# Layer 0 of a two-layer macaron kernel: the product delta times u on GpSimd, in four pieces of 256 columns

## The chip, the cores and the metric

The kernel runs on one core of a Trainium2 chip. A core has five engines with a queue each: TensorE (PE; its weight loads are shown as PEld), VectorE (DVE), ScalarE (ACT), GpSimd (POOL) and SyncE (SP), which here issues DMA transfers. Each engine takes the instructions of its queue in order and waits, with everything behind, until what the next instruction needs is ready. The metric is the device time of one launch in microseconds (us); less is better. Times of single instructions come from one execution that the hardware profiler recorded.

## The reference

Input `x` has 4 sequences of 1024 tokens with 128 features. Layer 0 is a mixture of experts, a selective state-space block and the mixture again; layer 1 is a mixture, an attention with 16 modulations and the mixture again. The part that matters here is the state-space block of layer 0:

```python
u = jax.nn.silu(u)                                  # after a convolution over 3 tokens
x_dbl = u @ W_x
dt, Bm, Cm = jnp.split(x_dbl, [DT_RANK, DT_RANK + D_STATE], axis=-1)
delta = jax.nn.softplus(dt @ W_dt + b_dt)
deltaA = jnp.exp(jnp.einsum('bld,dn->bldn', delta, A))
deltaB_u = jnp.einsum('bld,bln->bldn', delta * u, Bm)
...
h = dA * h + dbu                                    # along the 1024 tokens
y = jnp.einsum('bdn,bn->bd', h, c)
...
y = y + u * D_param
```

There are 4 sequences `b`, 256 inner features (two halves `c` of 128, one per partition) and 16 states `n`. The product `delta * u` depends on `b` and `c` only; it is made eight times and used by 16 states each.

## The kernel before

All of layer 0 is written under a manual schedule: the order in which the Python code issues instructions is the order in every queue. The work is cut into small generators ("pieces"), and a loop of 128 ticks, one for each (b, c, n), advances each piece a step and then does the recurrence of its tick.

A tick `t` consists of these steps, all on tiles of 128 partitions and 1024 columns (tokens):

- `inflow(t)`, GpSimd, L484: `hs = du * row_b`, in four operations of 256 columns. It is issued `AHEAD` = 5 ticks ahead by `total`, and `hs` has six buffers, so an `hs` can be written once PE has read the tile of six ticks ago. Behind it SP loads the row of `Bm` for tick t + 3, spread over 128 partitions (512 KB).
- `decay(t)`, ScalarE, L493: `da = exp(delta * A)`, into the one PSUM tile of that name; it has to wait until the scan of the tick before has read it.
- `state(t)`, VectorE: the scan L499 along the tokens (reads `da` and `hs`), then L503, the product with the row of `Cm`; SP loads the next such row behind it.
- `total(t)`, PE, L512: adds `hs` to the sum `y` over the 16 states, through a product with the identity.
- `skip(b, c)`, VectorE, L523, after the 16 states: `u * D + y`.

Between the ticks run the other pieces. `mixtures` computes the mixture of experts, one expert a step: PE makes `hp` (L359), ScalarE `r` (L325), GpSimd multiplies `r` by the routing weights `m_w` in two operations of 256 columns (L332), ScalarE squares it to `h` (L342), PE multiplies `h` by the second weights (L349). Where a tick advances that piece twice, two of each stand there. `others` does gates and routing; its `route_rows` and `normed` are chains of small VectorE operations on 8 columns (`rsqrt`, L81 to L87). `following` prepares the next sequence: `prepare(b)` makes `u`, and `softplus(b, c)` makes `delta` in steps of ScalarE and VectorE (L432 to L460) and ends with `du` (L461). For the second half c = 1 it waits until the last tick of the sequence before. `following` is advanced before `mixtures`, and both before `total` and `state` of the tick.

For the first sequence both `softplus(0, 0)` and `softplus(0, 1)` run before the loop, beside the mixture of sequence 1; after them the first five `inflow` and the first `decay` are issued, then the ticks.

`delta` and `du` have two buffers each. `delta` is read by `decay` and by the product `du`; `du` is read by `inflow` alone. GpSimd's queue in layer 0 holds L332, L484, the gate products L538, and some fills at the start.

Of the kernel before, what the change touches and what calls it, by code (L numbers as in the profile page):

```python
# [22 lines left out]
ALU = mybir.AluOpType  # L23
# [4 lines left out]
B, L, C = 4, 1024, 128  # L28
# [132 lines left out]
def layer0(tc, k):  # L161
# [15 lines left out]
    nc = tc.nc  # L177
# [11 lines left out]
    with (  # L189
# [194 lines left out]
        u, x_rows, xd, delta, du = {}, {}, {}, {}, {}  # L384
# [41 lines left out]
        def softplus(b, c):  # L426


            v = sb.tile([P, L], F32, name="sp_v", bufs=1)
            for half in range(3):  # L430
                if half > 0:
                    nc.scalar.activation(  # L432
                        v[:, ts(half - 1, HL)], pdt, AF.Identity, bias=k.b_dt[:, c : c + 1]
                    )
                if half < 2:
                    pdt = ps_t.tile([P, HL], F32, name="pdt", tag="tr")
                    nc.tensor.matmul(
                        pdt,
                        k.w_dt[:, ts(c, P)],
                        xd[b][0:DTR, ts(half, HL)],  # L440
                        start=True,
                        stop=True,
                    )
                yield
            z = sb.tile([P, L], F32, name="sp_z", bufs=1)
            nc.vector.scalar_tensor_tensor(z, v, -1.0, v, op0=ALU.mult, op1=ALU.min)
            yield
            nc.scalar.activation(z, z, AF.Exp)
            yield
            w1 = sb.tile([P, L], F32, name="sp_w", bufs=1)  # L450
            nc.vector.tensor_scalar(w1, z, 1.0, None, op0=ALU.add)
            nc.vector.scalar_tensor_tensor(z, w1, -1.0, z, op0=ALU.add, op1=ALU.subtract)
            yield
            nc.scalar.activation(w1, w1, AF.Ln)
            nc.vector.scalar_tensor_tensor(v, v, 0.0, z, op0=ALU.max, op1=ALU.subtract)
            yield
            yield from until(lambda: c == 0 or now >= b * DI * NS - 1)
            delta[b, c] = sb.tile([P, L], F32, name="delta")
            du[b, c] = sb.tile([P, L], F32, name="du")
            nc.vector.tensor_tensor(delta[b, c], v, w1, op=ALU.add)  # L460
            nc.vector.tensor_tensor(du[b, c], delta[b, c], u[b][:, c, :], op=ALU.mult)  # L461
            yield


# [120 lines left out]
        def until(ready):  # L585
            while not ready():
                yield
# [26 lines left out]
        def following():  # L614

            for b in range(1, B):
                yield from until(lambda: now >= (b - 1) * DI * NS and {1, b} <= mixed)
                yield from prepare(b)
                yield from softplus(b, 0)
                yield from softplus(b, 1)  # L620

        def first():
            yield from prepare(0)
            yield from softplus(0, 0)
            yield from softplus(0, 1)
# [972 lines left out]
```

## Time and profile before

| what | value |
|---|---|
| device time, median of 3 runs | 8004.84 us (8004.07 to 8005.69) |
| profiled execution, device time | 8007.9 us |
| its span, first to last instruction | 8006.1 us |
| granted TensorE clock, mean | 0.963 |
| PE, DVE, ACT, POOL busy share of the span | 84%, 86%, 91%, 11% |
| first and last start of a scan's decay (L493) | 162.4 and 945.2 us |
| L484 on GpSimd, 512 operations: min, median, max | 712, 723, 1795 ns |
| L461 on VectorE, 8 operations: min, median, max | 1226, 1594, 1633 ns |
| L460 on VectorE, 8 operations: min, median, max | 1218, 1628, 1744 ns |

The span is the profiled execution's time from its first to its last instruction; the device time of the same execution has the launch around it. A row of costly groups gives the source line, the engine, the operation, the tile written and the tiles read, the number of instructions, then busy time in us and the mean of one in ns, and last the idle time of the engine just before them with what ended it. A row of the timeline gives the start in us, the length in us, the engine, the line and the operation; operations that follow each other without a gap are merged and counted ("x4"), and a bracket shows idle time before and what ended it. A row of the waits gives the waiting engine with its tile and line, what it waited for, then the total in us, the number of times and the longest. The eight `delta` (L460) start at 146.5, 161.7, 315.3, 370.6, 515.0, 577.3, 710.1 and 758.8 us. Busy time by stretches of 100 us:

| stretch, us | PE | DVE | ACT | POOL |
|---|---|---|---|---|
| 100 to 200 | 66.41 | 50.61 | 50.21 | 58.31 |
| 300 to 400 | 77.24 | 84.29 | 53.84 | 81.29 |
| 500 to 600 | 77.06 | 79.96 | 56.97 | 80.56 |
| 700 to 800 | 74.27 | 81.18 | 54.55 | 81.99 |
| 1200 to 1300 | 85.15 | 88.92 | 100.00 | 2.40 |

### The profile page before, as it was taken

The page shows a single profiled execution, that of the slowest core. Times are in us where ns is not written, and L with a number is a line of the kernel's source. Part 1 is how long each engine was busy: PE and PEld are TensorE (multiplying, and loading weights), DVE is VectorE, ACT ScalarE, POOL GpSimd, SP SyncE. Part 2 cuts the span into 40 slices and gives each one's busy share as a digit, 9 for nine tenths or more (in the row PEclk, how much of TensorE's full clock was granted, in tenths as well). Part 3 has the DMA queues.
Part 4 walks back from the last instruction along what each step waited for, and adds up shares of the span by engine and source line. Part 5 has one row for each costly group of instructions (what it writes and reads, how often), then busy time and mean ns, then how long its engine had stood idle before and what let it go on. Part 6 is the DMA issues. An engine that isn't in the chain of part 4 may idle for free. (4 is left out here: it accounts for less than half of the span.)

```text
span 8006.1 us, 169674 instructions
## 1 busy us (share of the span) xinstructions
PE 6750.8 (84%) x76154; PEld 3048.4 (38%) x76154; DVE 6919.1 (86%) x11239; ACT 7292.7 (91%) x1800; POOL 863.6 (11%) x1025
## 2 busy tenths in 40 slices
PE   6777778888888888888888888888888888888885
PEld 3443343333333333333333333333333333333333
DVE  4878668898988999888899898888899989888886
ACT  4555449999999999999999999999999999999995
POOL 4777610000000000000000000000000000000000
PEclk8988879999999999999999999999999999999997
DMA  3556400000000000000000000000000000000001
GB/s 118 193 190 195 155 27 1 2 1 1 2 2 1 2 2 1 2 2 2 1 2 1 2 2 2 1 2 2 1 1 1 2 1 2 1 2 1 2 1 32
DMA packets 71789, 192.09 MB, mean 24 GB/s; under 512 B 9848, under 2 KB 19840, under 8 KB 71040
## 3 DMA queue, kind: packets, MB, share of 16 engines
q1 hardware_dynamic: 66736, 178.38, 6.9%
q8 instruction: 604, 9.90, 0.5%
q10 hardware_dynamic: 4304, 2.62, 0.1%
q14 instruction: 145, 1.19, 0.0%
HBM read 176.91 MB, written 4.06 MB: 23 GB/s over the span
## 5 line engine op out<-in xcount | busy, mean ns | idle before, releaser
L1276 ACT ACTIVATE p_w<-xs,cc 128x7680 f32<-128x7680 f32 x1024 | 6747.8, 6713 | 23.3 <-PE o L1287 23.3
L1287 PE MATMUL o<-p_w,vt 128*9 128x256 f32 x61440 | 3791.6, 385 | 777.0 <-ACT p_w L1276 776.1
L1287 PEld LDWEIGHTS o<-p_w,vt 128*9 128x9 f32 x61440 | 1772.2, 92 | 2723.4 <-ACT p_w L1276 1216.5
L1062 DVE TENSOR_REDUCE nm<-s 128x1 f32<-128x1024 f32 x512 | 624.5, 1220 | 281.8 <-PE s L1048 280.6
L1114 DVE SCALAR_TENSOR_TENSOR x_m<-p_s,x_m 128x512 f32<-128x512 f32 x1024 | 708.5, 692 | 35.6
L1115 DVE SCALAR_TENSOR_TENSOR x_m<-x_m,p_s 128x512 f32<-128x512 f32 x1024 | 708.6, 692 | 34.9
L1116 DVE SCALAR_TENSOR_TENSOR p_s<-x_m,x_z 128x512 f32<-128x512 f32 x1024 | 708.5, 692 | 34.9
L1113 DVE SCALAR_TENSOR_TENSOR p_s<-x_m 128x512 f32<-128x512 f32 x1024 | 700.7, 684 | 0.0
L1085 DVE COPY xs<-s 128x1024 f32<-128x1024 f32 x508 | 608.4, 1218 | 98.5 <-PE s L1048 98.2
L1143 POOL TENSOR_TENSOR rz<-rz,iw_c 128x128 f32<-128x128 f32 x64 | 26.0, 407 | 5732.9 <-DVE rz L1142 5732.9
L1287 PE MATMUL o<-p_s,vtop 128*9 128x256 f32 x4096 | 623.5, 383 | 9.7 <-DVE vtop L1124 9.7
L1048 PE MATMUL s<-kp,qp 32*128 32x512 f32 x2048 | 581.4, 644 | 0.7 <-DVE nm L1062 0.7
L1048 PE MATMUL s<-qp,kp 32*128 32x512 f32 x2048 | 549.4, 634 | 0.8 <-ACT xs L1085 0.8
L1101 DVE TENSOR_SCALAR x_z<-xs,cc 128x512 int32<-128x512 f32 x1024 | 522.7, 510 | 1.1
L1105 DVE TENSOR_SCALAR x_m<-x_z 128x512 int32<-128x512 int32 x1024 | 437.7, 427 | 35.3
L1108 DVE TENSOR_SCALAR x_z<-x_z 128x512 int32<-128x512 int32 x1024 | 437.6, 427 | 35.3
L484 POOL TENSOR_TENSOR hs<-du,row_b 128x256 f32<-128x256 f32 x512 | 438.1, 888 | 112.3 <-PE y L512 103.2
L499 DVE TENSOR_TENSOR_SCAN hs<-da,hs 128x1024 f32<-128x1024 f32 x128 | 292.2, 2283 | 89.9 <-ACT da L493 74.4
L512 PE MATMUL y<-hs,ident 128*128 128x512 f32 x512 | 287.6, 692 | 97.1 <-DVE hs L503 71.3
L1319 DVE COPY os<-o 128x512 f32<-128x512 f32 x512 | 348.7, 681 | 10.1 <-PE o L1287 9.1
L1132 PEld LDWEIGHTS pt<-ident,os 128*128 128x128 f32 x2048 | 214.2, 140 | 368.2 <-issue 118.8
L493 ACT ACTIVATE da<-delta,neg_a 128x1024 f32<-128x1024 f32 x128 | 142.7, 1115 | 229.1 <-DVE hs L499 228.7
(228 smaller groups left out, 4343.9 us busy)
## 6 DMA issues: line engine op xcount, KB each, us to landing
row_b<-x_rows SPq DMA_DIRECT2D x128, 512.0 KB
row_c<-x_rows SPq DMA_DIRECT2D x128, 512.0 KB
m_w<-m_rows SPq DMA_DIRECT2D x128, 256.0 KB
x_sb<-in_L_attn_x_dram ACTq DMA_DIRECT2D x4, 512.0 KB
c_w<-in_L_ffn_w_dram SPq DMA_DIRECT2D x4, 512.0 KB
out_dram<-x_sb SPq DMA_DIRECT2D x4, 512.0 KB
c_b<-in_L_ffn_b_dram SPq DMA_DIRECT2D x2, 512.0 KB
xnt<-xs SPq DMA_DIRECT2D x2, 512.0 KB
```

The source lines that it names most:

```text
L484: nc.gpsimd.tensor_tensor(hs[t][:, part], du[b, c][:, part], rows_b[t][:, part], op=ALU.mult)
L1048: nc.tensor.matmul(s[:, ts(half, 512)], a[row, ts(i, P)], c[row, ts(half, 512)], start=True, stop=True,)
L1062: nc.vector.tensor_reduce(nm[:, i, 0:1], score(j, qp[n], i, kp[n]), AX.X, ALU.max, negate=True)
L1085: copy(xs[u][:, i, :], score(j, kp[n], i, qp[n]))
L1101: nc.vector.tensor_scalar(z, s, c, 127.0 * (1 << 23), op0=ALU.mult, op1=ALU.min)
L1105: nc.vector.tensor_scalar(m, z, 0x7FFFFF, 0x3F800000, op0=ALU.bitwise_and, op1=ALU.bitwise_or)
L1113: nc.vector.scalar_tensor_tensor(w, m, EXP2[0], m, op0=ALU.add, op1=ALU.mult)
L1114: nc.vector.scalar_tensor_tensor(m, w, EXP2[1], m, op0=ALU.add, op1=ALU.mult)
L1115: nc.vector.scalar_tensor_tensor(m, m, EXP2[2], w, op0=ALU.add, op1=ALU.mult)
L1116: nc.vector.scalar_tensor_tensor(p_s[g][:, 0:n], m, EXP2[3], e, op0=ALU.add, op1=ALU.mult)
L1276: nc.scalar.activation(p_w[:, n_s - min(SOFT) :], xs[u].rearrange("p a b -> p (a b)")[:, n_s:], AF.Exp, scale=cc[:, h, wl : wl + 1],)
L1287: nc.tensor.matmul(o[32 * r : 32 * r + D + 1, :], vtop[u] if soft else vts[b % 2][:, i, h, :], p_s[g][:, at : at + QW] if soft else p_w[:, ...
```

## The change

The product `du` leaves VectorE's queue and stands at the same place of the program on GpSimd, in four operations of 256 columns.

```diff
             delta[b, c] = sb.tile([P, L], F32, name="delta")
             du[b, c] = sb.tile([P, L], F32, name="du")
             nc.vector.tensor_tensor(delta[b, c], v, w1, op=ALU.add)
-            nc.vector.tensor_tensor(du[b, c], delta[b, c], u[b][:, c, :], op=ALU.mult)
+            for q in range(4):
+                part = ts(q, L // 4)
+                nc.gpsimd.tensor_tensor(
+                    du[b, c][:, part], delta[b, c][:, part], u[b][:, c, part], op=ALU.mult
+                )
             yield
```

VectorE's queue loses eight instructions and GpSimd's gains 32; the order of all others is the same on every engine. In GpSimd's queue the first `du` stands before the product of the last expert of sequence 1's mixture, and the second stands behind that product and before the first `inflow`. The `du` of c = 0 and c = 1 of the later sequences stand between the `inflow` of two ticks; at c = 1 of sequences 1 and 2 and at c = 0 of sequence 1 the products of two experts (L332) follow at once, at c = 1 of sequence 3 the product of one, and at c = 0 of sequences 2 and 3 an `inflow`. Lines after L461 lie four further down in the changed kernel, where the new product is L463.

## The prediction

> **What bounds the kernel now.** I read the page first, then the waits of 300 to 900 us, then the timeline around each of the eight places where `du` is made. The page puts the long stage after 1,200 us under ScalarE (L1276, 6747.8 us of 8006.1); the change does not touch it, and it starts when layer 0 is done. So only layer 0 counts, and in it the 128 ticks between 168 and 949 us.
>
> The costliest groups, two of them in layer 0 (busy, mean ns | idle before, releaser), and the line that goes:
>
> ```profile
> L484 POOL TENSOR_TENSOR hs<-du,row_b 128x256 f32<-128x256 f32 x512 | 438.1, 888 | 112.3 <-PE y L512 103.2
> L499 DVE TENSOR_TENSOR_SCAN hs<-da,hs 128x1024 f32<-128x1024 f32 x128 | 292.2, 2283 | 89.9 <-ACT da L493 74.4
> ```
>
> ```profile
> L461 DVE TENSOR_TENSOR du<-delta,u x8: 1226/1594/1633, 147.7 to 760.7; 128x1024 f32<-128x1024 f32 x8
> ```
>
> GpSimd runs ahead until the ring of six `hs` is full (it idles for PE `y`), so its product for a tick is early by about four ticks. VectorE idles most for the decay `da`, that is for ScalarE. What holds ScalarE up shows in the waits:
>
> ```profile
> ACT da L493 <- DVE hs L499: 181.4, 60, 8.9
> ...
> POOL hs L484 <- PE y L512: 80.0, 24, 8.6
> ...
> ACT h L342 <- POOL r L332: 49.8, 25, 4.4
> ...
> DVE hs L499 <- ACT da L493: 48.7, 18, 5.6
> ```
>
> The third row matters: ScalarE's queue is in order, `h` stands ahead of the next `da`, and `h` waits for GpSimd's product `r` (L332). A late GpSimd reaches the scan by r, h, da, scan, although its `hs` are early.
>
> **Prices.** A GpSimd product of 256 columns undisturbed takes 0.69 us (four in 2.77), a pair 1.40. VectorE's 1024-column product takes 1.23 alone; where the two meet, GpSimd's four take 3.75 (+0.98) and VectorE's one 1.4 to 1.74. Small VectorE operations show it best:
>
> ```profile
> 309.49 0.65 DVE L85 SCALAR_TENSOR_TENSOR rq<-rs 128x8 f32<-128x8 f32 x1
> ...
> 312.12 2.77 POOL L484 TENSOR_TENSOR hs<-du,row_b 128x256 f32<-128x256 f32 x4
> ...
> 314.26 0.65 DVE L86 TENSOR_TENSOR rq<-rq,tot 128x8 f32<-128x8 f32 x1
> 314.94 0.17 DVE L87 SCALAR_TENSOR_TENSOR rs<-rq,rs 128x8 f32<-128x8 f32 x1
> ```
>
> 0.65 us while GpSimd multiplies, 0.17 as soon as it stops: one small operation passes per GpSimd operation, 0.68 apart in place of 0.20, so 0.48 is lost on each.
>
> **The change, part by part.** Removed from VectorE: eight L461, 12.4 us in all. Added to GpSimd: 32 products, 32 x 0.69 = 22.2 us. Nothing else moves in any queue, and no DMA is added; but GpSimd's `du` now waits for `delta` (VectorE), and behind it wait the `r` and `hs` of the following ticks, and SP's loads of `row_b`, which follow `hs`.
>
> *Start (two places).* The rows, and the scan that follows:
>
> ```profile
> 151.26 22.75 POOL L484 TENSOR_TENSOR hs<-du,row_b 128x256 f32<-128x256 f32 x24
> ...
> 161.73 1.56 DVE L460 TENSOR_TENSOR delta<-sp_v,sp_w 128x1024 f32<-128x1024 f32 x1
> ...
> 163.32 1.63 DVE L461 TENSOR_TENSOR du<-delta,u 128x1024 f32<-128x1024 f32 x1
> ...
> 168.05 2.27 DVE L499 TENSOR_TENSOR_SCAN hs<-da,hs 128x1024 f32<-128x1024 f32 x1
> ```
>
> Six ticks of `hs` are made from 151 on, while VectorE is still busy with the second delta. In the new queue the second `du` stands before the first `hs`. The first `du` (149.1 to 151.9) delays the last `r` of the mixture, its `h` and ScalarE's work for the second delta by 2.0; with GpSimd then idle, four VectorE steps (L446, L452, L455, L460) fall from 1.52, 1.63, 1.63, 1.56 to about 1.22, -1.5. Delta ends at 163.85 (was 163.29), `du` at 166.65, the first `hs` at 169.45: the first scan at 169.5, +1.45. Then the lead is missing: eight `hs` blocks from 166.65 take 8 x 2.77 and 2 x 0.98 for two L503, to 190.8. The layer norm's 24 small VectorE operations (179.1 to 186.1 in the profile, 5 of them slow) now begin at 180.8 and meet GpSimd: 15 at 0.68 and 9 at 0.20 end at 192.8. Shift +6.7; after that both engines stand as before. Ends: +1.45 if none more is slowed, 1.45 + 19 x 0.48 = +10.6 if all are. I take 6.7, since the row at 309 to 315 shows exactly this. That loads of `row_b` come later (169.5 for use at about 176; in the profile 154.05 for 162.7) lies inside these ends.
>
> *Second halves, c = 1 (371, 577, 759 us).* The first of them:
>
> ```profile
> 370.23 4.74 POOL L484 TENSOR_TENSOR hs<-du,row_b 128x256 f32<-128x256 f32 x4
> ...
> 374.93 3.76 POOL L332 TENSOR_TENSOR r<-r,m_w 128x256 f32<-128x256 f32 x4
> ...
> 376.37 0.63 ACT L342 ACTIVATE h<-r 128x512 f32<-128x512 f32 x1 [3.48 <-POOL r L332]
> ...
> 376.90 1.10 ACT L493 ACTIVATE da<-delta,neg_a 128x1024 f32<-128x1024 f32 x1
> ```
>
> Here GpSimd is the late one. Without L461 its `hs` ends 0.98 earlier (373.99); `du` takes 2.77 and 0.98 for the L503 it meets, to 377.74; `r`, `h`, `da` come 2.8 later. VectorE is 1.6 early, waits for `da`, and starts its scan at 380.9 in place of 378.94; the skip after it (L523) waits for PE, which waits for `h`: +2.9. The place at 577 has the same rows: +2.9. At 759: `r` +2.8, scan +1.4, the next `r` and with it skip about +2.5. Sum +8.3 (2.0 to 2.9 each).
>
> *First halves, c = 0 (315, 515, 710 us).* Here GpSimd is early. At 515 and 710 it stands idle until delta, so the L503 and delta before it fall from 1.49 and 1.74 to 1.23; with L461 (1.63) gone the scan starts 2.3 earlier, `da` and the table loads behind it too; `du` and the late `hs` are four ticks ahead of need: -2.1 and -1.9. At 315, GpSimd idles from 309.4, the eight slow small operations save 8 x 0.48 = 3.8 and delta ends at 312.7; then `du`, two `r`, `hs` fill GpSimd to 322.1, the next `r` (321.76 in the profile) is no earlier, and of 1.8 only 0.7 stays. Sum -4.7 (ends -6.0, and 0 if `r` behind `du` eats all).
>
> Sum: 6.7 + 8.3 - 4.7 = **+10.3 us**; lower ends 1.45 + 6.0 - 6.0 = +1.5, upper 10.6 + 8.7 + 0 = +19.3. Against the profiled execution: span 8006.1 to 8016.4, with its launch (8007.9) to 8018.2; the median lies 3.1 under that, so 8004.84 + 10.3 = **8015.1**.
>
> The row prices four products at 2.77 us. The Trainium skill (GPSIMD Engine Reference, "Elementwise — side-by-side cycle accounting") gives 4.5 us for a product of 2048 columns, thus an estimate of 2.25 for 1024; with five `du` on the path (two at the start, three c = 1) the sum would be 5 x 0.52 lower, +7.7. No trace here shows one product of 1024 columns on GpSimd. The row of 3.75 beside 2.77 has a rule too (Trace Analysis, "Optimizing Scalar/DVE Operations"): GpSimd and VectorE share a port, and moving work between them may not help. Taken strictly it strikes out the gains at c = 0, and the sum is +15.0; the trace speaks against taking it so, since GpSimd stands idle there before delta.
>
> **Rivals.**
> 1. *GpSimd is the bound wherever it works for the experts, and pays in full.* Each of the six places in the loop costs 2.8, as `r` behind `du` holds ScalarE's `h` and `da`, and nothing of L461 comes back: 6 x 2.8 + 6.7 = +23.5, 8028. It decides as soon as `r` ends later than the scan that frees `da`. For it: 49.8 us of `h` waiting for `r`, and at 315 it eats most. Against: at 515 and 710 no expert product comes for 10 and 12 us (`r` at 526.95 and 728.29).
> 2. *VectorE is the bound, and GpSimd's lead hides all.* -12.4 for L461: 7992; with the slowed deltas and small operations (about -8) 7984. For it: 80.0 us of GpSimd waiting for `y`. Against: the start, where no lead exists yet, and the c = 1 rows.
> 3. *The change does nothing*, `du` being hidden both ways: 8005. Against: each c = 1 row has `h` waiting for GpSimd already.
>
> **How the numbers follow.** From no change this kernel can be told by about 0.2%, 16 us: 7988.8 and 8020.8. My sum 0.50 and rival 3 0.05, both within; rival 1 and mixtures near it 0.38 (slower); rival 2 0.07, of which 0.02 within and 0.05 faster. Same 0.57, slower 0.38, faster 0.05. The range runs from 8003, 3.5 below the lower end for some of rivals 2 and 3, to 8030, over rival 1; the forecast's own is 8006 to 8024.
>
> **What would show it.** Start: first scan near 169.5, the second layer norm's small operations at 0.65 until about 190, third scan near 192.8. At c = 1: `h` after `du` 2.8 later relative to delta's start, the scan waiting for `da`. At c = 0: GpSimd idle until delta, 1024-column delta at 1.23, the scan right behind it. Wrong if GpSimd's `du` are well above 0.69 each, if the third scan comes before 188, or if the c = 0 places lose time.

## The result, and the profile after

| | before | changed |
|---|---|---|
| median of 15 runs each, us | 8005.58 (7998.71 to 8011.31) | 8020.03 (8015.08 to 8024.63) |
| profiled execution, span, us | 8006.1 | 8018.2 |

The ratio is 1.0019, with a 95% interval of 1.0012 to 1.0025: 14.5 us slower, between 10 and 20. Forecast were +10.3 and a range of 8003 to 8030.

The same groups of the page, and the new line by its source (count: min/median/max in ns, first and last start):

```profile
L488 POOL TENSOR_TENSOR hs<-du,row_b 128x256 f32<-128x256 f32 x512 | 422.1, 857 | 109.8 <-PE y L516 108.0
...
L503 DVE TENSOR_TENSOR_SCAN hs<-da,hs 128x1024 f32<-128x1024 f32 x128 | 292.2, 2283 | 100.2 <-ACT da L497 82.6
```

```profile
L463 POOL TENSOR_TENSOR du<-delta,u x32: 712/722/1712, 148.4 to 774.5; 128x256 f32<-128x256 f32 x32
```

The 32 products cost what the row priced. The scan's idle time grew from 89.9 to 100.2 us, of it 82.6 for `da` (74.4 before). The waits of 300 to 900 us; the row of `h` was the point:

```profile
ACT da L497 <- DVE hs L503: 166.1, 57, 11.0
...
DVE hs L503 <- ACT da L497: 65.8, 23, 5.2
ACT h L342 <- POOL r L332: 63.1, 24, 7.1
...
POOL du L463 <- DVE delta L460: 10.1, 3, 3.4
```

`h` waits 13 us longer for `r`, the scan 17 us longer for `da`; the new wait is there, 10.1 us of GpSimd for delta, at the three c = 0 places alone.

**Where the time went.** I set the 128 scans of both traces side by side (start in the changed kernel less start before) and then four later points. Ticks count from 0. A "power" is one of the 1024 exponentials that ScalarE makes in the attention.

| point | shift, us |
|---|---|
| first scan; third scan | +1.1; +5.8 |
| tick 20; 25 (past sequence 1, c = 0) | +6.4; +4.5 |
| tick 36 (past sequence 1, c = 1) | +10.2 |
| tick 53; 55 (past sequence 2, c = 0) | +10.2; +8.2 |
| tick 64; 65; 68 (past sequence 2, c = 1) | +9.0; +15.6; +10.0 |
| tick 85; 90 (past sequence 3, c = 0) | +8.8; +6.4 |
| tick 95; 100 (past sequence 3, c = 1) | +5.3; +8.7 |
| last scan | +5.3 |
| first power of the attention (ScalarE, L1280) | +5.7 |
| end of its last | +3.2 |
| first layer-norm row of the last mixture (L95) | +9.7 |
| end of the span | +12.1 |

So less than half of the 12.1 us of these two profiles is in layer 0. Of the rest, 6.5 us arise between the end of the last power and the row of L95, in one wait of VectorE. (Another 2.4 arise behind that row, about what the attention had gained before it, 2.5; the second profile of the changed kernel, below, does not have them.) From VectorE's waits, before and changed:

```profile
DVE ln_st L95 <- issue: 2.4, 1, 2.4
```

```profile
DVE ln_st L95 <- issue: 8.9, 1, 8.9
```

"Issue" is time in which the engine waited for nothing that the profile shows. The two parts are taken one after the other.

**The start** went as worked out. The changed kernel's timeline:

```profile
163.66 2.77 POOL L463 TENSOR_TENSOR du<-delta,u 128x256 f32<-128x256 f32 x4 [11.11 <-DVE delta L460]
166.39 23.79 POOL L488 TENSOR_TENSOR hs<-du,row_b 128x256 f32<-128x256 f32 x32
169.19 2.29 DVE L503 TENSOR_TENSOR_SCAN hs<-da,hs 128x1024 f32<-128x1024 f32 x1 [2.42 <-POOL hs L488]
...
189.56 0.64 DVE L85 SCALAR_TENSOR_TENSOR rq<-ln_rstd 128x8 f32<-128x8 f32 x1
190.24 0.17 DVE L86 TENSOR_TENSOR rq<-rq,ln_a 128x8 f32<-128x8 f32 x1
...
191.92 2.28 DVE L503 TENSOR_TENSOR_SCAN hs<-da,hs 128x1024 f32<-128x1024 f32 x1
```

GpSimd multiplies without a gap to 190.18, and the layer norm's small operations run at 0.65 until just then.

**c = 1** did not. Sequence 1, around the skip (L527) that follows the second scan:

```profile
378.38 3.75 POOL L463 TENSOR_TENSOR du<-delta,u 128x256 f32<-128x256 f32 x4
...
382.09 2.77 POOL L332 TENSOR_TENSOR r<-r,m_w 128x256 f32<-128x256 f32 x4
383.52 0.63 ACT L342 ACTIVATE h<-r 128x512 f32<-128x512 f32 x1 [6.19 <-POOL r L332]
...
385.25 2.29 DVE L503 TENSOR_TENSOR_SCAN hs<-da,hs 128x1024 f32<-128x1024 f32 x1 [3.46 <-ACT da L497]
...
390.29 5.53 POOL L488 TENSOR_TENSOR hs<-du,row_b 128x256 f32<-128x256 f32 x8
390.55 1.28 DVE L527 SCALAR_TENSOR_TENSOR u<-u,c_d_param,y 128x1024 f32<-128x1024 f32 x1 [3.01 <-PE y L516]
...
391.75 5.14 DVE L507 TENSOR_TENSOR hs<-hs,row_c 128x1024 f32<-128x1024 f32 x1
```

`du`, `r`, `h`, `da`, scan is the predicted chain, with the predicted late scan. But then L507, 1.2 to 1.8 us at all but three ticks, takes 5.14. It ends at 396.89; GpSimd's unbroken eight products end at 395.82, 1.07 earlier. VectorE was held out until GpSimd paused. At tick 64 the same takes 7.06, at tick 96 4.33. In the kernel before, the same product at tick 32 took 1.71, also behind the skip with GpSimd at work, but at tick 96 it was long there too:

```profile
383.54 1.71 DVE L503 TENSOR_TENSOR hs<-hs,row_c 128x1024 f32<-128x1024 f32 x1
...
775.35 3.21 DVE L503 TENSOR_TENSOR hs<-hs,row_c 128x1024 f32<-128x1024 f32 x1
```

**c = 0** went as worked out. Sequence 2:

```profile
524.90 1.22 DVE L460 TENSOR_TENSOR delta<-sp_v,sp_w 128x1024 f32<-128x1024 f32 x1
...
526.04 2.28 DVE L503 TENSOR_TENSOR_SCAN hs<-da,hs 128x1024 f32<-128x1024 f32 x1
...
526.20 2.77 POOL L463 TENSOR_TENSOR du<-delta,u 128x256 f32<-128x256 f32 x4 [3.41 <-DVE delta L460]
```

Delta takes 1.22 (1.74 before), the scan is right behind it, GpSimd waits 3.41 for delta and delays nobody.

### The profile page after: what moved, and what is told of

It is laid out like the page before. It is cut to its first block, busy times and chain, and to the rows that moved or that the text cites. A ratio compares the mean times of both kernels' runs of the same rounds, so it can differ in the third digit from the quotient of the medians.

```text
span 8018.2 us, 169699 instructions
## 1 busy us (share of the span) xinstructions
PE 6751.3 (84%) x76154; PEld 3047.9 (38%) x76154; DVE 6911.2 (86%) x11231; ACT 7292.2 (91%) x1800; POOL 869.6 (11%) x1057
## 5 line engine op out<-in xcount | busy, mean ns | idle before, releaser
L1280 ACT ACTIVATE p_w<-xs,cc 128x7680 f32<-128x7680 f32 x1024 | 6747.9, 6694 | 20.8 <-PE o L1291 20.7
L503 DVE TENSOR_TENSOR_SCAN hs<-da,hs 128x1024 f32<-128x1024 f32 x128 | 292.2, 2283 | 100.2 <-ACT da L497 82.6
```

What stands on the lines that cost most here:

```text
L1280: nc.scalar.activation(p_w[:, n_s - min(SOFT) :], xs[u].rearrange("p a b -> p (a b)")[:, n_s:], AF.Exp, scale=cc[:, h, wl : wl + 1],)
```

## The experiments

There are three groups of four kernels, each group with its own 33 runs of the kernel before on the same chip. Times are differences between the median of 11 runs and the median of these 33; "last scan" is that scan's start in the run's profile less 946.4. Layer 0 is not the same to the microsecond in two executions, as the first experiment shows.

**The kernel before again**, no edit.

> The kernel before, unchanged, as a second profile and as the noise floor. If VectorE's wait before the last mixture's first L95 (2.4 us in the profile before, 8.9 in the changed kernel's) belongs to the program, it is 2.4 +- 1 here again and the time is within 4 us of before. If it is chance of an execution, it lies elsewhere in 2 to 9. In layer 0 every scan starts within 1 us of the profile before.

Time +2.1 us (ratio 1.0001, 0.9992 to 1.0010). The wait before L95 is 2.4 again. Layer 0 is less steady than expected: scans are within 2 us up to tick 68, then up to 4.9 late, and the last is 1.7 early. So a shift of under 5 us in the middle of layer 0 of one profile says nothing by itself, and one ratio of 11 runs leaves some 7 us either way. A step between two close ticks that recurs in several kernels says more. One such step is nobody's doing here: from tick 100 to the last scan this repetition loses 3.7 us, and all the other twelve profiles lose 0.7 to 3.7 as well, so that much of each "last scan" belongs to the first profile of before.

**One kind of place at a time.** The edit of the first kernel; the second has `b > 0 and c == 0` there, the third `b > 0 and c == 1`:

```diff
-            for q in range(4):
+            if b == 0:
+                for q in range(4):
...
+            else:
+                nc.vector.tensor_tensor(du[b, c], delta[b, c], u[b][:, c, :], op=ALU.mult)
```

> Only the two du of sequence 0 on GpSimd. Theory: the missing lead costs once, third scan at 191.9 in place of 186.1, and the 5.8 us stay to the end of layer 0 (last scan +5 to +7). Rival, the lead is regained and the loss with it: the shift is under 2 us by the 20th scan. Rival of rivals 1 (GpSimd is the bound and pays in full): 8 products add 5.5 on GpSimd and scans go on slipping after the third.

> Only the three du of c = 0 of sequences 1 to 3 on GpSimd. Theory: a gain at each, -2.0, -1.6, -1.9 us (as the changed kernel's scans show), together -5 to -6 at the last scan. Rival (GpSimd pays in full): +2.8 at each, +8.4. Third view, gains are given back at once by later waits: within 1.5 of zero.

> Only the three du of c = 1 of sequences 1 to 3 on GpSimd. Theory: h behind r behind du, and VectorE's L503 behind the skip held out while GpSimd multiplies without a gap: +5.4, +1.5, +1.8 where they happen, +6 to +9 at the last scan. The prediction's working: +2.9, +2.9, +2.5, +8.3, without a long L503. Rival (du is hidden): under 2 us.

| on GpSimd | time, us | ratio, interval | shift of scans |
|---|---|---|---|
| start alone | +5.2 | 1.0005, 0.9996 to 1.0014 | third +6.4, tick 94 +6.3, last +1.2 |
| c = 0 alone | -6.4 | 0.9990, 0.9981 to 0.9999 | tick 25 -1.1, 64 -5.5, 90 -7.7, last -13.3 |
| c = 1 alone | +12.9 | 1.0014, 1.0005 to 1.0023 | third 0.0, tick 36 +7.0, 68 +10.8, 100 +11.8, last +9.0 |

The signs are those of the theory, and those of the prediction. The start's loss holds for some 90 ticks; 2.7 of it is given back at tick 96, where the long product of before (3.21) is absent, and 2.4 in the last ticks, where every profile loses some; that only +1.2 is left there is against what I expected. Its time alone does not tell it from no change. c = 0 alone gains at each place (-1.9, -2.0, -1.7; in the seven other profiles with these three on GpSimd at the same places the steps are -1.5 to -2.5, in the repeated kernel before 0.1 at most). Its last scan is earlier than the theory allowed: of the -13.3, 5.6 are these places, 2.7 the long product of tick 96, absent here too, and 2.7 the last ticks; the rest is not accounted for, and the time shows -6. c = 1 alone has the long product each time (its line is L510 there, the skip's L530):

```profile
387.11 5.52 POOL L491 TENSOR_TENSOR hs<-du,row_b 128x256 f32<-128x256 f32 x8
388.24 1.28 DVE L530 SCALAR_TENSOR_TENSOR u<-u,c_d_param,y 128x1024 f32<-128x1024 f32 x1 [3.88 <-PE y L519]
389.44 4.27 DVE L510 TENSOR_TENSOR hs<-hs,row_c 128x1024 f32<-128x1024 f32 x1
```

The rival "GpSimd pays in full at each place" falls with c = 0, "hidden" with c = 1. The three times add to +11.7; all three kernels have the short wait before L95.

**Eight more VectorE instructions, in the changed kernel.**

```diff
             nc.vector.tensor_scalar(neg_a, neg_a, -1.0, None, op0=ALU.mult)
+            pad = cst.tile([P, NS], F32, name="pad")
+            for _ in range(8):
+                nc.vector.tensor_scalar(pad, neg_a[:, 0, :], -1.0, None, op0=ALU.mult)
```

> The changed kernel with eight small VectorE operations (16 columns, into a tile that nobody reads) ahead of the first mixture, so that VectorE has as many instructions as before. If the 8.9 us before the last mixture's first L95 come from where VectorE's instructions lie, the wait is 2.4 again and the time 4 to 7 us under the changed kernel's (+8 to +10 over before). If it comes from the moment or from chance, it is 8.9 or anything, and the time stays +14. The scans of layer 0 move by under 1.5 us, the start's by what the eight take.

Time +10.9 (1.0013, 1.0004 to 1.0022). The wait before L95 is 2.2. The shift of the scans differs from the changed kernel's by more than I had allowed (first scan +3.2 against +1.1, last +9.3), so the time is no clean measure. Whether the eight did that is not shown, as the changed kernel's second profile (below) has its first scan at +4.3 without them. The next attempt puts them behind the ticks.

**The skip behind the product**, in the changed kernel.

```diff
-            if t > 0 and tick[t][2] == 0:
-                skip(*tick[t - 1][:2])
             nc.vector.tensor_tensor(hs[t], hs[t], rows_c[t], op=ALU.mult)
+            if t > 0 and tick[t][2] == 0:
+                skip(*tick[t - 1][:2])
```

> The changed kernel, with the skip (L527) behind the product with row_c (L507) of the same tick instead of ahead of it. Theory: L507 was held out for 5.14, 7.06 and 4.33 us behind the skip at ticks 32, 64 and 96; ahead of the skip it takes 1.3 to 1.8, the skip, which reads PSUM, takes its 1.28 at once, and the time falls by 5 to 10 us against the changed kernel. Rival, the long L507 only fills a wait that ScalarE's da makes anyway: under 2 us, and the scans behind then wait for da.

Time +7.8 (1.0011, 1.0002 to 1.0020), against +14.5 and, repeated below, +12.6 of the changed kernel in other groups; last scan -3.3 against +5.3. The same stretch in its profile:

```profile
388.27 1.80 DVE L505 TENSOR_TENSOR hs<-hs,row_c 128x1024 f32<-128x1024 f32 x1
...
391.34 1.28 DVE L527 SCALAR_TENSOR_TENSOR u<-u,c_d_param,y 128x1024 f32<-128x1024 f32 x1 [1.28 <-PE y L516]
391.98 8.54 POOL L488 TENSOR_TENSOR hs<-du,row_b 128x256 f32<-128x256 f32 x11
```

The product (L505 in this kernel) takes 1.80, the skip its 1.28 at once though GpSimd multiplies, and no product in the run takes over 1.9. From tick 32 to 33 and from 64 to 65 the shift of the scans grows by less than 0.4, where it grows by 5.3 and 6.7 in the changed kernel. So the long product was on the path. By the medians the edit takes 5 to 7 us away; the intervals of the times overlap, so its size is not settled.

**The six later `du` behind the experts' products**, without and with that edit (`late` collects (b, c) where `softplus` made the product; sequence 0 is on VectorE).

```diff
...
             if now > 0:
                 total(now - 1)
+            while late:
+                product(*late.pop())
             state(now)
```

> The two du of sequence 0 on VectorE as before; the six later ones on GpSimd, but issued behind the experts' products and the inflow of their tick. Theory: without du ahead of r the c = 1 places lose nothing, and VectorE's 1.6 us come back: -2 at each of the six, -8 to -14 at the last scan. Rival (GpSimd's work costs wherever it stands, as it delays the next r by 2.8): +5 to +9 as with c = 1 alone.

> Both changes together. Theory: their gains add, -12 to -20 us against before. Rival, both remove the same wait: no better than the better of the two alone.

Time -1.3 (0.9998, 0.9989 to 1.0007) and -4.1 (0.9994, 0.9985 to 1.0003); last scan -3.4 and -8.2. Both miss: better than the changed kernel (the start's loss is out of both, too), but no clear gain on before. In the first, `du` at 378.71 stands ahead of the next tick's `r`, and that `h` waits 5.24: the delay was moved by a tick. That is the rival's mechanism, though its +5 to +9 did not come; and at tick 96 a product takes 6.49. In the second, no skip stands ahead of a product, yet the one behind the scan of tick 97 takes 6.54.

**The changed kernel again**, no edit, and **with eight VectorE instructions behind the ticks:**

```diff
         skip(B - 1, 1)
+        for _ in range(8):
+            nc.vector.tensor_scalar(neg_a[:, 0, :], neg_a[:, 0, :], -1.0, None, op0=ALU.mult)
```

> The changed kernel, unchanged, as a second profile. If VectorE's wait of 8.9 us before the last mixture's first L95 belongs to the program, it is 6 to 10 again, and from the end of the last decay-and-power activation of the attention to the end of the span it takes 6 to 9 us more than before; if it was chance, 2 to 3 in this one. Layer 0: last scan +3 to +8, the three long L507 again.

> The changed kernel with eight small VectorE operations behind the loop of ticks, on a tile that is no longer read, so that VectorE has as many instructions as before and the ticks are those of the changed kernel. Code theory: the wait before L95 is 2 to 3 and the time 5 to 8 us under the changed kernel's of this call. Rival, the wait depends on when the stage begins and not on the number of instructions: 6 to 10 as in the changed kernel.

Again: +12.6 (1.0017, 1.0008 to 1.0026); last scan +6.6, long products 4.96, 6.29, 4.15. With the eight: +8.6 (1.0011, 1.0002 to 1.0020); last scan +6.6 too. VectorE's wait in the one and in the other:

```profile
DVE ln_st L95 <- issue: 7.5, 1, 7.5
```

```profile
DVE ln_st L95 <- issue: 2.2, 1, 2.2
```

Over all fourteen profiles: 7.5, 7.6, 8.0 and 8.9 us in the four whose VectorE has 8 instructions fewer than before; 2.2 to 2.5 in the ten with 0, 2, 3 or 6 fewer, two of these being the changed kernel with eight put back at two different places. From the end of the last power to L95, the four take 4.1 to 6.5 us more than before; the two with eight put back, 0.2 less. In the other seven kernels with the short wait it differs from before by 0.2 at most. The time fell by 4.0 with the eight, less than the 5 to 8 expected, and within what two such medians differ by.

The Trainium skill (Runtime: NRT & Kernel Launch, "Instruction fetch mechanics") has an engine's instructions fetched in blocks of 256 while it executes, mostly hidden. A block that comes late would fit a wait that depends on the count, but no run here shows the fetch itself.

**One `du` in one piece**, in the changed kernel.

```diff
-            for q in range(4):
-                part = ts(q, L // 4)
-                nc.gpsimd.tensor_tensor(
-                    du[b, c][:, part], delta[b, c][:, part], u[b][:, c, part], op=ALU.mult
-                )
+            nc.gpsimd.tensor_tensor(du[b, c], delta[b, c], u[b][:, c, :], op=ALU.mult)
```

> The changed kernel with each du as one GpSimd operation of 1024 columns. By the rows (0.69 us for 256) it takes 2.7; by the page's 4.5 us for 2048 columns 2.25. If VectorE's two-input operations wait for the whole GpSimd operation that is running, L507 beside it waits up to 2.7 and GpSimd is not stretched to 3.75. Time within 5 us of the changed kernel's.

Time +8.5 (1.0012, 1.0003 to 1.0021), against +12.6 of the changed kernel in the same group; the intervals overlap. A piece takes 2.34 us, and VectorE's product beside it waits:

```profile
377.77 2.34 POOL L461 TENSOR_TENSOR du<-delta,u 128x1024 f32<-128x1024 f32 x1
378.09 3.10 DVE L503 TENSOR_TENSOR hs<-hs,row_c 128x1024 f32<-128x1024 f32 x1
```

0.32 us into GpSimd's operation, VectorE's (here L503) starts, and ends 1.08 after it: it waited for the whole. The Trainium skill (SBUF — State Buffer, "SBUF: two separate sides") says so: of a VectorE operation with two SBUF inputs and a GpSimd operation the first to start has the port pair for its whole length. This row agrees. By that rule alone four pieces would let VectorE in after at most 0.7 us; the 5.14 of L507 beside pieces of 0.69 does not agree. The 4.5 us that the Trainium skill (GPSIMD Engine Reference, "Elementwise — side-by-side cycle accounting") gives for 2048 columns is for an addition; half of it, 2.25 for 1024 as an estimate, is close to the 2.34.

This kernel also shows that standing behind the skip is not what decides. At tick 64 the product starts as far into GpSimd's operations as in the changed kernel, 0.87 and 0.88 us behind the start of the row, and behind the same skip. First the changed kernel, then this one:

```profile
598.52 2.77 POOL L488 TENSOR_TENSOR hs<-du,row_b 128x256 f32<-128x256 f32 x4
599.39 7.06 DVE L507 TENSOR_TENSOR hs<-hs,row_c 128x1024 f32<-128x1024 f32 x1
```

```profile
597.04 3.77 POOL L484 TENSOR_TENSOR hs<-du,row_b 128x256 f32<-128x256 f32 x4
597.92 1.62 DVE L503 TENSOR_TENSOR hs<-hs,row_c 128x1024 f32<-128x1024 f32 x1
```

Over all fourteen profiles a product behind the skip, with a GpSimd operation running as it starts and the next one following at once, was held out in 20 cases of 66, and behind a scan in one of some 1000 beside pieces of 256 columns.

**c = 0 alone, and the skip behind the product:** both edits above on one kernel.

> Only the three du of c = 0 of sequences 1 to 3 on GpSimd, and the skip behind the product with row_c. Theory: the gains of c = 0 stay (-6 to -13 at the last scan) and the long operation behind the skip at tick 96 of the kernel before (3.2 to 4.2) is gone: -8 to -16 us against before in the time. Rival: the skip's place was worth nothing there, as with the first halves alone (-6).

Time 7995.6, -10.6 us (0.9988, 0.9979 to 0.9997); last scan -12.2, no product over 1.9 us. It is the fastest of the kernels, and its whole interval lies under 1, as that of c = 0 alone just does. Against c = 0 alone (-6.4, another group) the intervals overlap, and that kernel has no product over 1.9 us either, its last scan at -13.3: there was no long product left for the moved skip to remove. That the move gains anything here is not shown.

## Why the prediction was right, and where not

The time lies in the range, 4.9 us over the point, and slower by 0.18%, inside the 0.2% that held most of the chance. The total is nearer than its steps.

- *Price of the 32 products, 0.69 us, and GpSimd's stretch to 3.75 beside VectorE:* as said (2.75 to 3.76 for four).
- *Start, +6.7:* right. First scan 169.19 (169.5 said), third 191.92 (192.8), the small operations slow until 190.2 (190.8). When the start was changed alone, the shift stayed to tick 96 (+6.3) and not to the end.
- *c = 0, -4.7:* right in sign and mechanism; in the changed kernel -1.9, -2.0 and -2.4 across the three places, with -0.7, -2.1 and -1.9 said. At 315 the gain was kept where I had most of it eaten. (The expert product that rival 1 lacks at 710 is further off than I wrote: 728.29 is 16.4 us behind delta's end, not 12.)
- *c = 1, +8.3:* the chain was right up to the scan (385.25 against 378.94 is 6.3, of which 4.5 were there before; +1.9 said). The step that failed is the price "VectorE's one 1.4 to 1.74" where it meets GpSimd. It came from places where VectorE slips in between two products; at these three it did not, and L507 took 5.14, 7.06 and 4.33. The skip put behind the product took that away. A row of it was in the trace before, 3.21 at tick 96, and I read past it. At tick 64 most of the loss came back at once: in the changed kernel the layer norm's small operations behind the long product met an idle GpSimd (0.17 each, 0.65 before), and +15.6 fell to +10.0. Across the three places the shift grew by 5.7, 1.9 and 2.3, 9.9 in all, where I had 8.3.
- *Layer 0's sum, +10.3:* +5.3 in the first profile, +6.6 in the second, +6.6 with the eight late instructions; against the second profile of before +6.9, +8.3 and +8.3. So it is too high by 2 to 5, which is no more than two profiles of one kernel differ by.
- *"So only layer 0 counts":* failed. Eight fewer VectorE instructions cost 4.1 to 6.5 us some 7 ms later, before the last mixture. No step had it, and it filled what layer 0's sum had too much: that the total came so near is in part luck.

Rival 1 (pays in full at each place) and rival 2 (GpSimd's lead hides all) each hold for half of the six places in the loop: c = 1 costs in sum what rival 1 says (9.9 against three times 2.8), though more than that at the first place and less at the others; c = 0 gains what rival 2 says. What stays open: why the wait before L95 depends on VectorE's instruction count (that it does is shown, at 8 fewer; where its instructions come from at that moment is not), and why VectorE's product gets in behind the skip at one time and is held out at another.

## What to carry to other kernels

Moving work to an engine with idle time pays only where that engine stands idle at that moment and what is queued behind the moved work has slack: the same edit gained at c = 0 and lost at c = 1 and at the start, and only the selective versions, with c = 0 alone, came out below the kernel before with their whole interval, by 0.1%. Look for a VectorE operation with two SBUF inputs that takes far longer than elsewhere while GpSimd multiplies without a pause, and try another order there: in the changed kernel, with the one that reads PSUM behind it, it was gone. When instruction counts change, compare the stages far behind the change too.

## What the runs showed of the hardware that was not expected

- A VectorE product of 1.2 us can be held out for as long as GpSimd's products follow each other without a gap: beside pieces of 256 columns 3.2 to 7.1 us in 21 cases over ten of the profiles, all but one right behind the skip, and each ended 1.08 or 1.09 us after a GpSimd operation behind which GpSimd stood idle for 3.3 us or more. Elsewhere, and behind the skip in 46 cases too, it was done in 1.2 to 1.8 us. What decides between the two is not known: the order of the two operations alone does not, nor does how far GpSimd is when the product starts.
- A GpSimd product of 1024 columns took 2.34 us in one piece, four of 256 columns 2.77.
- VectorE's wait of 2.2 to 2.5 us in front of the last mixture was 7.5 to 8.9 in every kernel with exactly eight VectorE instructions fewer, and in none of the others.
